# Two mixture-of-experts layers in one kernel: the second on gapless tiles of tokens, the first with a reordered start and earlier transposes

## The chip, the cores and the metric

The kernel runs on one core of a Trainium2 chip. Its time is device microseconds of one execution; before the change it is 2235.64 us, the median of three runs (2235.45 to 2235.82). A core has five engines that work side by side, each on a queue of its own: TensorE (PE in the profile; its weight loads are listed apart as PEld), VectorE (DVE), ScalarE (ACT), GpSimd (POOL) and SyncE (SP), which here only issues DMAs. A "q" behind an engine's name means its queue, where waits, register loads and DMA issues are handled.

## What is computed

The reference is a graph network of two layers over 2500 tokens of 256 features. Each layer adds a graph convolution and an attention block to the tokens and ends in a mixture of eight experts. What the change touches are the two expert parts:

```
# layer 0: each token takes its two best experts, unweighted
xn = layernorm(x)
idx = top_k(xn @ Wg + bg, 2)
h = gelu(einsum('td,edh->teh', xn, W1) + b1)          # W1: 8 x 256 x 512
y = einsum('teh,ehd->ted', h, W2) + b2                # W2: 8 x 512 x 256
x = x + sum of y over the two chosen experts

# layer 1: one shared first product, then one expert of eight
H = gelu(layernorm(x) @ W1 + b1)                      # W1: 256 x 1024
probs = softmax(H @ Wg + bg); e = argmax(probs)
x = x + probs[e] * (H @ Wd[e] + bd[e])                # Wd: 8 x 1024 x 256
```

All products are float32.

## The kernel before

Tokens lie on chip in `X`, 125 partitions by 20 blocks by 260 columns: 256 features and four columns for small facts such as mean, scale and the token's number. Five groups of four blocks (`NG`, `GT`) are the unit of most loops. Python writes the program in an order; a framework then orders the instructions on each engine's queue by their dependencies and by its own idea of when they are ready, so an instruction can stand earlier on its queue than the program has it. On the chip every queue is worked off in order.

**First expert layer.** `gates0(g, ...)` is a generator in three parts: statistics and normalized rows (lines 505 to 515), transposes and the choice of two experts (517 to 530), and slots and scatter (532 to 535). It runs for group g beside the aggregation of group g+1 (lines 664 to 701); for the last group all three parts run after the loop (711, 712). `take_slots` counts, with two small matmuls, how many tokens of each expert came before and so gives each token a row in the table `sorted0`, where each expert has a region of its own; `scatter` writes the rows with one indirect DMA of POOL for each block and choice (line 403). A fallback for lost edges follows as a loop of zero or one turns (line 715), which on these inputs is not entered but which every engine must pass. After it `pad` writes 128 empty rows behind each expert's tokens (eight DMAs of SP, line 491), and `plan` works out on VectorE which expert and which row each of the 47 tiles of 128 rows has (lines 414 to 436). Then, for each tile, `hidden` loads weights (`wt`) and rows (`xs`), transposes them into `px`, copies these to `xc`, forms the hidden products and the gelu `h`; `rest` forms the second product `py`, adds, and scatters to `back0`. The loop at lines 791 to 797 runs `hidden` one tile ahead of `rest`.

**Last expert layer.** A first pass (`gates`, `route`) forms H for all tokens, uses it for the gate alone, and scatters the rows by expert to `sorted1`. `pad` and `plan` follow as above, for 27 tiles: 20 would hold 2500 rows, and each of eight experts may leave its last tile partly empty. The second pass takes tiles in groups of three (`TG`): load, normalize to `xh`, transpose, eight products of 384 columns with gelu (lines 1256 to 1260), then for each tile eight products with its expert's matrix (line 1265), the sum `yo`, and an indirect DMA to the output (line 1271). Rows that are empty carry an index beyond the output and are dropped.

Of the kernel before, what the change touches and what calls it, by code (L numbers as in the profile page):

```python
# [10 lines left out]
I32 = mybir.dt.int32  # L11
# [28 lines left out]
NS1 = -(-N // TS) + NE - 1  # L40
# [8 lines left out]
def gps_kernel(ctx: ExitStack, tc: tile.TileContext, a, out):  # L49
# [45 lines left out]
    X = xpool.tile([P, NT, RW], F32, tag="X", name="X")  # L95
# [25 lines left out]
    slots = const.tile([P, NS0], F32, name="slots")  # L121
# [4 lines left out]
    region = const.tile([P, NE], F32, name="region")  # L126
# [241 lines left out]
    def one_best(pool, onehot, s):  # L368

        best = pool.tile([P, GT], F32, tag="best", name="best", bufs=2)  # L370
        V.tensor_reduce(best, s, AX.X, ALU.max)
        key = pool.tile([P, GT, NE], F32, tag="key", name="key", bufs=2)
        V.tensor_tensor(key, s, best[:, :, None].to_broadcast([P, GT, NE]), ALU.is_equal)
        V.tensor_tensor(key, key, rev[:, None, :].to_broadcast([P, GT, NE]), ALU.mult)
        first = pool.tile([P, GT], F32, tag="first", name="first", bufs=2)
        V.tensor_reduce(first, key, AX.X, ALU.max)
        V.tensor_tensor(onehot, key, first[:, :, None].to_broadcast([P, GT, NE]), ALU.is_equal)

    def take_slots(pool, mask, fill):


        flat = mask.rearrange("p i e -> p (i e)")
        ps = psum2.tile([P, 2, GT, NE], F32, tag="cx", name="ps")
        T.matmul(ps[:, 0].rearrange("p i e -> p (i e)"), below, flat, start=True, stop=True)  # L384
        T.matmul(ps[:, 1].rearrange("p i e -> p (i e)"), ones[:, :P], flat, start=True, stop=True)  # L385
        slot = pool.tile([P, GT, NE], F32, tag="slot", name="slot", bufs=2)
        for k in range(GT):
            V.tensor_tensor(slot[:, k, :], ps[:, 0, k, :], fill, ALU.add)  # L388
            V.tensor_tensor(fill, ps[:, 1, k, :], fill, ALU.add)
        return slot  # L390

    def slot_of(pool, slot, mask):

        t = pool.tile([P, GT, NE], F32, tag="pick", name="pick", bufs=2)
        V.tensor_tensor(t, slot, mask, ALU.mult)
        to = pool.tile([P, GT], I32, tag="to", name="to", bufs=4)
# [4 lines left out]
    def scatter(table, to, rows, moved):  # L401
        for k in range(GT):
            moved.append(G.indirect_dma_start(  # L403
                out=table, out_offset=bass.IndirectOffsetOnAxis(ap=to[:, k:k + 1], axis=0),
                in_=rows[:, k, :], in_offset=None,
# [4 lines left out]
    def plan(pool, fill, ns):  # L410
# [3 lines left out]
        V.tensor_tensor(tiles, fill, region, ALU.subtract)  # L414
# [7 lines left out]
        V.tensor_tensor(of, last[:, None, :].to_broadcast([P, ns, NE]), slots[:, :ns, None].to_broadcast([P, ns, NE]), ALU.is_le)  # L422
        who = pool.tile([P, ns], F32, name="who")
        V.tensor_reduce(who, of, AX.X, ALU.add)
        expert = pool.tile([P, ns], I32, name="expert")
# [3 lines left out]
        V.scalar_tensor_tensor(tiles, tiles, -float(TS), region, ALU.mult, ALU.add)  # L429
# [4 lines left out]
        V.scalar_tensor_tensor(who, slots[:, :ns], float(TS), who, ALU.mult, ALU.add)  # L434
        begin = pool.tile([P, ns], I32, name="begin")
        V.tensor_scalar(begin, who, float(NE * CAP), None, ALU.min)
        return expert, begin
# [39 lines left out]
    sorted1 = dram.tile([NE * CAP + TS, RW], F32, name="sorted1")  # L477
    back0 = dram.tile([2 * N, D], F32, name="back0")

    for table in (sorted0, sorted1):  # L480
        nc.scalar.dma_start(table[NE * CAP:NE * CAP + TS, :], empty)

    def pad(pool, table, empty, fill, moved):

        ends = pool.tile([P, NE], I32, name="ends")
        V.tensor_copy(ends, fill)
# [12 lines left out]
    fill0 = const.tile([P, NE], F32, name="fill0")  # L499
    V.tensor_copy(fill0, region)  # L500
    fill1 = const.tile([P, NE], F32, name="fill1")
    V.tensor_copy(fill1, region)

    def gates0(g, pool, moved):

        mv, rstd = norm_stats(X, g * GT, GT)
        rows = [pool.tile([P, GT, RW], F32, tag=f"rows{n}", name=f"rows{n}", bufs=2 - n) for n in range(2)]
# [203 lines left out]
    for _ in range(3):  # L711
        next(gating)
# [626 lines left out]
```

## Time and profile before

| what | us |
|---|---|
| median of three runs | 2235.64 |
| profiled execution, whole | 2239.74 |
| its span, on which all rows below are | 2238.0 |
| TensorE busy | 2009.1 |
| VectorE busy | 872.0 |
| ScalarE busy | 594.2 |
| GpSimd busy | 294.4 |
| last update of X before the first expert layer ends | 304.09 |
| first transpose of the first expert layer | 354.94 |
| its last scatter starts | 548.84 |
| last scatter to `sorted1` starts | 2010.72 |
| first product of the second pass | 2022.33 |
| last expert product ends, last scatter starts | 2230.45, 2231.71 |

Times within the span are microseconds from its start. A float32 matmul shows as two records in the trace, so a count of x16 is eight matmuls. The row "PEclk" of the page gives the clock granted to TensorE, in tenths of full speed: after an idle stretch it is half for some microseconds.

### The profile page before, as it was taken

What the parts mean: (1) busy time and instruction counts of PE and PEld (TensorE: products, weight loads), DVE (VectorE), ACT (ScalarE), POOL (GpSimd) and SP (SyncE); (2) the same over time, 40 slices, a digit from 0 to 9 for tenths busy, and PEclk for the clock granted to TensorE, in tenths of its full rate; (3) what the DMA queues carried; (4) which work ended last, traced back from release to release, by engine and by line L of the source; (5) the groups of instructions that cost most, each with busy time, mean ns of one, the idle gap of its engine ahead of it and who ended that gap; (6) DMA issues with size and microseconds to landing.
All of it is one profiled execution on the core that took longest, in us unless ns stands there. A gap on an engine that the chain in (4) does not pass through costs nothing. (4 is left out here: it accounts for less than half of the span.)

```text
span 2238.0 us, 25483 instructions
## 1 busy us (share of the span) xinstructions
PE 2009.1 (90%) x9145; PEld 1336.2 (60%) x9145; DVE 872.0 (39%) x2764; ACT 594.2 (27%) x1008; POOL 294.4 (13%) x265
## 2 busy tenths in 40 slices
PE   2799956997799999999999999999987997978998
PEld 2556635876476766676666676767643442326676
DVE  7866532332734463434525463443120003222111
ACT  1533202222533323232233324133110001332221
POOL 2303331222210000100001010011111000120111
PEclk9799977999899999999999999999989998988999
DMA  4113256664410001100110001100025336011110
GB/s 119 37 55 105 78 155 188 206 188 152 105 51 14 1 12 51 42 1 5 45 35 23 1 12 49 47 1 1 1 75 152 86 90 203 19 42 38 31 30 20
DMA packets 87295, 143.51 MB, mean 64 GB/s; under 512 B 18898, under 2 KB 69056, under 8 KB 86402
## 3 DMA queue, kind: packets, MB, share of 16 engines
q1 hardware_dynamic: 71233, 117.01, 18.0%
q0 software_dynamic: 12832, 18.28, 2.9%
q10 hardware_dynamic: 3093, 6.46, 1.1%
q8 instruction: 77, 1.26, 0.2%
q14 instruction: 60, 0.49, 0.1%
HBM read 104.84 MB, written 38.81 MB: 64 GB/s over the span
## 5 line engine op out<-in xcount | busy, mean ns | idle before, releaser
L1089 PE MATMUL mm<-w,h 128*125 128x256 f32 x1280 | 286.1, 379 | 0.0
L1079 PE MATMUL mm<-xT,w 128*128 128x500 f32 x640 | 283.2, 584 | 0.0
L288 PE MATMUL pa<-piece,table 125*128 125x500 bf16 x1200 | 269.8, 378 | 13.5 <-DVE t L852 5.6
L1089 PEld LDWEIGHTS mm<-w,h 128*125 128x125 f32 x1280 | 239.0, 188 | 43.2 <-issue 9.2
L288 PEld LDWEIGHTS <-table 125*128 125x128 bf16 x1200 | 117.7, 99 | 144.5 <-issue 17.8
L1079 PEld LDWEIGHTS mm<-xT,w 128*128 128x128 f32 x640 | 119.3, 191 | 112.6 <-issue 102.2
L1082 ACT ACTIVATE h<-mm,bf 128x500 f32<-128x500 f32 x160 | 107.1, 677 | 231.5 <-PE mm L1079 231.1
L288 PE MATMUL pa<-edges,xb 125*128 125x500 bf16 x600 | 134.2, 377 | 1.7 <-ACT edges L662 1.7
L1074 POOL TENSOR_TENSOR tok<-tok,b 125x1024 f32<-125x1024 f32 x20 | 47.3, 2365 | 584.6 <-DVE tok L1066 534.1
L1090 DVE TENSOR_TENSOR tok<-tok,mm 125x256 f32<-125x256 f32 x80 | 33.5, 418 | 210.0 <-PE mm L1089 169.3
L1257 PE MATMUL mm<-xc,w 128*128 128x384 f32 x288 | 102.1, 511 | 7.5 <-DVE xc L92 5.4
L765 PE MATMUL mm<-xc,wt 128*128 128x128 f32 x752 | 97.1, 283 | 7.5 <-DVE idx L771 4.3
L765 PEld LDWEIGHTS mm<-xc,wt 128*128 128x128 f32 x752 | 89.6, 194 | 17.8 <-DVE xc L761 12.4
L779 PE MATMUL py<-w,h 128*128 x376 | 96.0, 381 | 0.9 <-ACT h L769 0.9
L288 PEld LDWEIGHTS <-xb 125*128 125x128 bf16 x600 | 58.1, 100 | 63.8 <-issue 3.9
L1265 PE MATMUL mm<-wd,hs 128*128 x432 | 94.7, 379 | 0.0
L1055 DVE TENSOR_TENSOR tok<-tok,po 125x256 f32<-125x256 f32 x80 | 30.2, 414 | 154.4 <-PE po L1052 153.9
L769 ACT ACTIVATE h<-mm,wt 128x128 f32<-128x128 f32 x188 | 53.8, 368 | 137.3 <-issue 127.1
L1265 PEld LDWEIGHTS mm<-wd,hs 128*128 128x128 f32 x432 | 82.1, 190 | 13.1
L353 ACT ACTIVATE xT<-mm,mixc 128x500 f32<-128x500 f32 x80 | 58.9, 767 | 114.0 <-PE mm L348 79.8
L662 ACT CAST edges<-mm 125x500 bf16<-125x500 f32 x100 | 64.6, 784 | 88.9 <-PE mm L659 88.9
L1257 PEld LDWEIGHTS mm<-xc,w 128*128 128x128 f32 x288 | 55.4, 198 | 50.9 <-DVE xc L92 10.8
(325 smaller groups left out, 2832.2 us busy)
## 6 DMA issues: line engine op xcount, KB each, us to landing
wt<-in_expert_in_dram SPq DMA_DIRECT2D x47, 514.0 KB
piece<-adj SPq DMA_DIRECT2D x100, 218.8 KB
xs<-sorted SPq DMA_DIRECT2D x74, 130.0 KB
w<-in_L_mix_W_dram SPq DMA_DIRECT2D x8, 1024.0 KB
wd<-in_L_ffn_Wd_dram SPq DMA_DIRECT2D x8, 1024.0 KB
w<-in_L_ffn_W_dram SPq DMA_DIRECT2D x8, 512.0 KB
adj<-edges SPq DMA_DIRECT2D x2, 1750.0 KB
terms<-t SPq DMA_DIRECT2D x10, 336.0 KB
```

What stands on the lines that cost most here:

```text
L288: T.matmul(pa[c], table[:, k, n, c * 128:(c + 1) * 128], e, start=(k == 0 and n == 0), stop=(k == NT - 1 and n == 2))
L353: S.activation(o, ps, AF.Identity, bias=shift[:, c:c + 1], scale=gain[:, c:c + 1])
L662: S.copy(o.rearrange("p s (n d) -> p n s d", d=BD), ps[:P].rearrange("p (n s d) -> p n s d", n=BD, d=BD))
L765: T.matmul(ps[:, j * TS:(j + 1) * TS], wt[:, c * F0 + j * 128:c * F0 + (j + 1) * 128], xc[:, c * TS:(c + 1) * TS], start=(c == 0), stop=(c ...
L769: S.activation(h[:, j * TS:(j + 1) * TS], ps[:, j * TS:(j + 1) * TS], AF.Gelu, bias=wt[:, 2 * F0 + j:2 * F0 + j + 1])
L779: T.matmul(ps, h[:, j * TS:(j + 1) * TS], w2[:, ds(e, 1), j, :], start=(j == 0), stop=(j == NJ - 1))
L1074: G.tensor_tensor(o, o, b2[:P, None, :].to_broadcast([P, GT, D]), ALU.add)
L1079: T.matmul(ps, w1[:, c, j * 128:(j + 1) * 128], fT[:, c, g * GC:(g + 1) * GC], start=(c == 0), stop=(c == 1))
L1082: S.activation(h, ps, AF.Gelu, bias=bf[:, l, j:j + 1])
L1089: T.matmul(ps, hh[j][:, k * P:(k + 1) * P], w2[:, j, :], start=(j == 0), stop=(j == nj - 1))
L1257: T.matmul(ps[:, :nt * TS], w1[:, c, j * 128:(j + 1) * 128], xc[:, c, :nt * TS], start=(c == 0), stop=(c == 1))
L1265: T.matmul(ps, hs[j][:, k * TS:(k + 1) * TS], wd[:, ds(e, 1), j, :], start=(j == 0), stop=(j == nj - 1))
```

## The change

In the first expert layer:

- The last group's gate is split into two generators of two blocks each. The first starts when the first two of the four blocks have their final X. The two are advanced by hand in the order 0, 1, 0, 1, 1.
- Both row buffers, `rows0` and `rows1`, now exist twice (before, `rows1` once). Filling the small columns and the copy to `rows1` move from the first part of `gates0` to the third, for all groups.
- `pad` and `plan` run ahead of the fallback loop; the loop repeats them for its own result. The load of the bias table `brow` moves from ACT's queue to SP's.
- `hidden` is cut in two: `turned0` loads, transposes and copies; it runs a whole tile ahead of the products.

In the last expert layer:

- `sorted1` has no regions with gaps. Pairs of experts share a stretch of 2500 rows, one filling it upwards and the other downwards (`sign`, `begin1`). The table lies in memory that held the adjacency, and there are no empty rows any more.
- `visits` replaces `pad` and `plan`. It gives each of 2500 places in order of expert its row (`whence`) and owner (`own`), and lists 27 visits: pairs of a tile and an expert with rows in it.
- The second pass runs over 20 tiles without gaps, 2500 columns, in groups of 2, 2, 4, 4, 4 and 4. `fetch` gathers rows with POOL's indirect DMA into X's own memory; `inner` writes the gelu into a ring of twelve tiles (`hs`). For each visit `take` copies one tile of the ring, at a place known only at run time, to `taken`, and `visit` multiplies by the expert's matrix. Rows of the tile that belong to another expert get an index beyond the output.

The core of the diff:

```diff
-        rows = [pool.tile([P, GT, RW], F32, ..., bufs=2 - n) for n in range(2)]
...
+    def gate_rows(pool):
+        return [pool.tile([P, GT, RW], F32, tag=f"rows{n}", name=f"rows{n}", bufs=2) for n in range(2)]
...
+                    if g == NG - 1 and k == 1:
+                        rows = gate_rows(gate0)
+                        halves = [gates0(g, gate0, moved0, rows, lo, 2) for lo in (0, 2)]
+                        next(halves[0])
+                if g < NG - 1:
+                    gating = gates0(g, gate0, moved0, gate_rows(gate0))
+                else:
+                    for b in (0, 1, 0, 1, 1):
+                        next(halves[b])
...
-    nc.scalar.dma_start(brow.rearrange("p e n -> p (e n)"), row_bcast(a["L0_ffn_b2"], 0, NE * D, 128))
-    for _ in range(3):
-        next(gating)
+    nc.sync.dma_start(brow.rearrange("p e n -> p (e n)"), row_bcast(a["L0_ffn_b2"], 0, NE * D, 128))
+    pad(moe, sorted0, empty, fill0, moved0)
+    expert, begin = (moe.tile([P, NS0], I32, name=name) for name in ("expert", "begin"))
+    plan(moe, fill0, NS0, expert, begin)
...
-    pad(moe, sorted0, empty, fill0, moved0)
-    expert, begin = plan(moe, fill0, NS0)
...
-    ahead = hidden(0)
-    for t in range(1, NS0):
-        nxt_t = hidden(t)
-        rest(*ahead)
+    queue = [turned0(0)]
+    ahead = None
+    for t in range(NS0):
+        if t + 1 < NS0:
+            queue.append(turned0(t + 1))
+        nxt_t = hidden(*queue.pop(0))
+        if ahead is not None:
+            rest(*ahead)
         ahead = nxt_t
```

The new second pass and the two functions it turns on (`inner`, `turned` and the ends of `visits` are left out):

```diff
+    def visits(pool, fill, at):
+        turned_by, start = (v.rearrange("p k t -> p (k t)") for v in (sign, begin1))
+        count = pool.tile([128, NE], F32, name="count")
+        V.tensor_tensor(count, fill, start, ALU.subtract)
+        V.tensor_tensor(count, count, turned_by, ALU.mult)
+        ends = pool.tile([128, NE], F32, name="ends")
+        V.tensor_copy(ends, count)
+        for e in range(1, NE):
+            V.tensor_tensor(ends[:, e:e + 1], ends[:, e:e + 1], ends[:, e - 1:e], ALU.add)
...
+        V.tensor_tensor(whence, place_of, side, ALU.add)
...
+        def fetch(lo, hi):
+            for t in range(lo, hi):
+                m = rows_of(t)
+                G.indirect_dma_start(
+                    out=xs[:m, t, :], out_offset=None, in_=sorted1,
+                    in_offset=bass.IndirectOffsetOnAxis(ap=whence[:m, t:t + 1], axis=0),
+                )
...
+        def take(v):
+            r = nc.values_load(kept[0:1, v:v + 1], engines=[mybir.EngineType.DVE], ...)
+            h = fin2.tile([128, nj * TS], F32, tag="taken", name="taken")
+            V.tensor_copy(h, hs[:, ds(r, 1), :].rearrange("p o n -> p (o n)"))
+            return v, h
+
+        def visit(v, h):
+            e = expert_of(expert, v)
+            r = nc.values_load(which[0:1, v:v + 1], engines=[mybir.EngineType.DVE], ...)
+            ps = psum2.tile([128, D], F32, tag="cx", name="py")
             for j in range(nj):
+                T.matmul(ps, h[:, j * TS:(j + 1) * TS], wd[:, ds(e, 1), j, :], start=(j == 0), stop=(j == nj - 1))
+            row = xs[:, ds(r, 1), :].rearrange("p o n -> p (o n)")
+            idx = fin2.tile([128, 1], I32, tag="idx", name="idx", bufs=4)
+            far = fin2.tile([128, 1], F32, tag="far", name="far", bufs=4)
+            V.tensor_scalar(far, own[:, ds(r, 1)], expert_f[:, v:v + 1], float(1 << 20), ALU.not_equal, ALU.mult)
+            V.tensor_tensor(idx, far, row[:, D + 3:D + 4], ALU.add)
+            yo = fin2.tile([128, D], F32, tag="yo", name="yo", bufs=4)
+            V.tensor_tensor(yo, ps, bdf[:, ds(e, 1), :].rearrange("p o n -> p (o n)"), ALU.add)
+            V.scalar_tensor_tensor(yo, yo, row[:, D + 2:D + 3], row[:, :D], ALU.mult, ALU.add)
...
+        fetch(*groups[0])
+        fetch(*groups[1])
+        xc, n = turned(*groups[0])
+        taken = None
+        for u, (lo, hi) in enumerate(groups):
+            inner(lo, hi, xc, n)
+            for v in range(lo, hi if u + 1 < len(groups) else NV):
+                nxt_v = take(v)
+                if taken is not None:
+                    visit(*taken)
+                taken = nxt_v
+                if v == lo and u + 1 < len(groups):
+                    xc, n = turned(*groups[u + 1])
+            if u + 2 < len(groups):
+                fetch(*groups[u + 2])
+        visit(*taken)
```

## The prediction

> **What bounds the kernel now.** I read the page first, then tables of busy time by stretch, the timeline of the two expert layers, and the waits inside them. The page's slices show TensorE at 90% of the span, with two dents that the change touches: slices 6 and 7 (280 to 392 us, digits 5 and 6) and slices 36 and 37 (from 1958 us, digits 7 and 8).
>
> ```profile
> PE   2799956997799999999999999999987997978998
> PEclk9799977999899999999999999999989998988999
> ...
> L1257 PE MATMUL mm<-xc,w 128*128 128x384 f32 x288 | 102.1, 511 | 7.5 <-DVE xc L92 5.4
> L765 PE MATMUL mm<-xc,wt 128*128 128x128 f32 x752 | 97.1, 283 | 7.5 <-DVE idx L771 4.3
> L1265 PE MATMUL mm<-wd,hs 128*128 x432 | 94.7, 379 | 0.0
> ```
>
> The reader should see that each expert layer is TensorE work of 90 to 100 us a line with little waiting in front of it. So two things pay: fewer columns, and shorter holes. The hole ahead of the first expert layer is seen in the timeline (start, duration, engine and line, operation; in brackets the idle time before it and what ended it):
>
> ```profile
> 303.61 0.48 DVE L700 SCALAR_TENSOR_TENSOR X<-mm,rval,X 125x256 f32<-125x256 f32 x1
> 312.70 1.04 ACT L515 COPY rows<-rows 125x1024 f32<-125x1024 f32 x1 [15.88 <-DMA sorted<-rows,to]
> 314.27 3.53 PE L522 MATMUL pg<-wg,gT 128*125 128x8 f32 x16 [4.05 <-ACTq L715]
> 335.20 1.18 POOL L403 DMA_INDIRECT sorted<-rows,to  x1 [0.30 <-issue]
> 341.40 0.17 DVE L486 CAST ends<-fill 125x8 int32<-125x8 f32 x1 [17.40 <-DMA piece<-adj]
> 342.28 6.65 SPq L491 DMA_DIRECT2D sorted<-empty  x8
> 351.18 0.36 SPq L756 DMA_DIRECT2D xs<-sorted  x1
> 354.94 0.69 PE L759 MATMUL px<-ident,xs 128*128 128x128 f32 x2 [33.07 <-DMA xs<-sorted]
> ```
>
> From the last update of X (304.09) to the first transpose (354.94) is a chain of 50.9 us: statistics, gate, eight scatters on POOL at 1.49 us each, the fallback loop at L715 that lets nobody on before the scatters have landed (341.2), then the plan, eight empty-row loads and the first tile. Inside the two layers TensorE waits for these (waits by engine and line, us in total, times, longest; first 360 to 548 us, then 2016 to 2238 us):
>
> ```profile
> PE mm L765 <- DVE idx L771: 4.3, 3, 1.7
> PE mm L765 <- DVE xc L761: 2.7, 3, 1.1
> PE py L779 <- ACT h L769: 0.9, 3, 0.3
> ```
>
> ```profile
> DVE idx L1267 <- DMA out_dram<-yo,idx: 50.4, 23, 4.4
> PE mm L1257 <- DVE xc L92: 5.4, 5, 2.4
> ```
>
> The second fence holds a trap: VectorE stands 50.4 us before `idx`, waiting for a scatter to give a buffer back, and now and then the copy of `xc` is queued behind it.
>
> **A, the head of the first expert layer.** Three edits. (1) The last gate runs in two halves of two blocks, and the first starts after block 1 instead of 3. VectorE's small operations cost about 0.2 us whatever their width: variance and rsqrt are 11 operations in 2.9 us (304.81 to 307.66), the choice of two experts 13 in 2.9 us (317.84 to 320.7), pick and index 0.7 us. Halving pays these 6.5 us twice. Against it: about 2 us of the first half's statistics fit into gaps before 304.09; TensorE's transposes and gate products (2.06 and 3.53 us at half clock) and the evacuations now lie beside VectorE; and POOL starts its first four scatters early. Added up: rows of half one 307.5, of half two 311; products of half one 311.3; its choice 314.3; slots, pick, index 317; four scatters 317.7 to 323.7. Half two has its index at about 321, before POOL is free, so its last scatter starts at 323.7 + 3 x 1.49 = 328.2 instead of 335.2: 7.0 us. (2) The second buffer of `rows1` takes away ACT's 15.88 us wait above, behind which the copy of `gT` stood (313.65 instead of 310.3); that is inside the 7.0. (3) Plan and empty rows move ahead of the loop. On SP they stand behind eight W2 loads, the bias load that moves there from ACT (0.4 us of issue) and seven `piece` loads, all issued by 320.3; eight empties at 0.83 us then end at about 328, beside POOL's scatters. The plan (5.5 us of VectorE) hides there too. The path from the loop's end to the first tile's load falls from 9.8 us (341.4 to 351.18) to two register loads and one weight load, 1.9 us as between 348.93 and 351.18 less 0.8 us of waiting: about 8 us. Together 15.0. Bounds: 7 if halving gains nothing or an empty row that lands late holds the loop; 17 if the order is ideal. I take 14, near the sum, as all terms but the interleaving are rows. If the `piece` loads were queued between the empties, some 1.5 us would be lost.
>
> Gates of groups 0 to 3 run beside the aggregation, where TensorE is full; their row setup moves behind the choice, POOL 0.66 us and ACT 1.04 us ahead of scatters nobody waits for: nothing. Two constants and one memset more at the start, one DMA fewer: nothing.
>
> **B, transposes a tile ahead.** TensorE needs 26 records a tile, 3.8 us (276 records from 400 to 440 us). It runs 188 us with 179.6 busy; the three waits above are 7.9 of the 8.4 idle. With `px` a tile (3.8 us) ahead, its evacuation (0.42 us) and the `idx` copy before it have that much slack. What is late next is the load of `xs`: its issue follows the weight buffer of four tiles back by some 4.4 us and it lands 3.7 to 4.1 us later, against a need at about 11.2 us: 2.7 us to spare. Bounds 4 to 8.3; I take 7.
>
> **C, the last expert layer.** Work removed: 27 tiles of 128 columns become 2500 columns. L1257 spaces its records 0.322 us for 384 columns (10.3 us for 32), 0.839 ns a column; 32 records a column make 92.7 us before, 67.1 after: 25.6. Transposes 54 to 40, at 0.137 us (0.82 us for six): 1.9. Expert products stay 27 x 16 records at 0.219 us, 94.5 us.
>
> Start: before, last scatter 2010.72, empties until 2015.0, `xs` issued 2016.80, first product 2022.33. After: `visits` costs VectorE some 25 small operations to `whence`, 5.2 us, done by 2011.2, hidden by the scatters. The gathers sit on POOL behind the scatters and need them landed, 4.0 us after issue, so about 2015; each costs 1.19 + 0.3 us on POOL and lands in 4.1 (the `win` gather). Two tiles land at 2019.2 and 2020.7, products at about 2022.3: even, 2 us either way.
>
> Stalls before: 2022.33 to 2230.45 is 208.1 us for 193.8 of work, so 14.3 lost (7.5 idle, the rest half clock). After I count: half clock 2.5; the first `take` exposed 2.5; the transposes of group 2, whose four gathers wait for the first visit's result, need 1 + 6 + 4 us and have 10.4 of cover, 2 with order; VectorE's queue 4; other 2: 13. Later groups have 13.75 + 3.5 us of cover for the same 11. New on VectorE per visit: three register loads at 0.30 us, `far` and `idx` 0.15 each, `yo` 0.42 + 0.48, and the copy `take` of 1024 elements, which the trace lacks. Nearest row: 1.22 us (L931, 1024 elements at one a cycle). The Trainium skill, "VectorE: DVE Perf Modes", perf-mode tier table, gives a float32 SBUF copy twice that rate, from which I estimate 0.7 us. Between 0.7 and 1.25 I take 1.1, by the row. Sum 3.2 us beside TensorE's 3.5 a visit: it just fits.
>
> A rule speaks against this copy: "SBUF — State Buffer", SBUF: two separate sides, says that such a copy locks POOL out of the port with which it writes descriptors. The trace has POOL's indirect DMAs at 0.97 us with no such copy beside them, landing 2.4 us after issue. By the row a scatter costs its visit nothing; by the rule it may land up to one copy (1.1 us) later. Only where the next `idx` waits for that landing does it reach TensorE: 21 visits without cover x 1.1 = 23 us by the rule, 0 by the row. I take the 4 us above.
>
> C gives 27.5 + 14.3 - 13 = 28.8; I take 28. Bounds 12 to 39.
>
> **Sum.** 14 + 7 + 28 = 49. The profiled execution (span 2238.0, 2239.74 in all) becomes about 2190.7; it lies 4.1 above the median of the runs, 2235.64, so I forecast **2187**.
>
> **Rivals.**
> 1. *The loop or SP holds the head, or the gathers pace the tail* (A 7, C 12 to 20): 2235.6 - 7 - 7 - 15 = about 2207. For it: eight empties share SP with 13 other loads. Against: DMA share falls to 0.15 after 324 us.
> 2. *VectorE's queue takes the bound in C; slower.* If each `idx` waits for the scatter of the visit before, as in the 50.4 us above, the cycle is `yo` 0.95, POOL 0.25, landing 2.5 + 1.1 by the lock, `idx` 0.3, `take` with loads 1.6: 6.7 us instead of 3.5. 21 visits x 3.2 = 67 us, less the 4 counted: 2187 + 63 = 2250. It decides from a cycle of 5.8 us (49 / 21 + 3.5). Against: `take` can be queued before that `idx`; then the cycle is 4.0.
> 3. *Everything overlaps*: A 17, B 8, C 36: 2175.
>
> **Chances.** Forecast (2176 to 2198) 0.55; rival 1 and milder forms of 2 (2198 to 2231) 0.27; rival 3 0.10; no change 0.02; rival 2 0.06. A measurement here tells 0.2%, 4.5 us, from nothing. Faster 0.92, same 0.02, slower 0.06. Range 2170 to 2214: rival 3 below, most of rival 1 above.
>
> **What would show it.** First `px` at about 341 instead of 354.94, last L403 scatter near 328; TensorE idle inside the first layer under 2 us; the 128x384 group replaced by 512- and 256-wide ones with 67 to 70 us; visits 3.5 us apart at the end. Wrong: a first `px` after 347, visits over 4.5 us apart, or VectorE waiting for `out_dram` with TensorE waiting for `taken`.

## The result, and the profile after

The changed kernel takes **2210.59 us**, the median of four runs (2205.23 to 2213.28), beside 2235.73 us of the kernel before in the same comparison: a ratio of 0.9884, with a 95% interval of 0.9863 to 0.9906. The gain is 25 us, about half of the 49 forecast. The time lies inside the range 2170 to 2214 and near the first rival's 2207.

The profiled execution takes 2208.22 us, with a span of 2205.4. That is 31.5 us less than the profiled execution before, which was itself 4.1 us above its median, while this one is 2.4 below: the traces differ by 6.5 us more than the medians do. I split the difference of the spans at three events found in both traces: the first transpose and the last scatter of the first expert layer, and the start of the last product that forms H for the gate (`mm<-xTf,w`), ahead of the second pass. The table calls this one the last gate product:

| stretch, us | before | after | gain |
|---|---|---|---|
| start to the first transpose of the first expert layer | 354.9 | 346.5 | 8.4 |
| from there to that layer's last scatter | 193.9 | 198.7 | -4.8 |
| from there to the last gate product (nothing is edited here) | 1447.3 | 1442.8 | 4.5 |
| from there to the end of the span | 241.9 | 217.4 | 24.5 |

So the last layer brings nearly all of it. The first layer starts 8.4 us earlier and gives more than half of that back before it ends. These are the rows of the page of the changed kernel that answer to those shown before:

```profile
PE   2799967998699999999999999999987897995997
...
L1394 PE MATMUL py<-wd,taken 128*128 x432 | 100.1, 390 | 8.8 <-DVE taken L1384 8.8
L851 PE MATMUL mm<-xc,wt 128*128 128x128 f32 x752 | 97.5, 283 | 10.2 <-DVE xc L841 8.8
...
L863 PE MATMUL py<-w,h 128*128 x376 | 94.2, 380 | 0.0
```

Two numbers matter. L851, the hidden product of the first layer, waits 10.2 us in all, 8.8 of them for the copy of `xc`; before, with the transposes in the same tile, its row had 7.5 in all. And L1394, the expert product of the last layer, waits 8.8 us for `taken`, an operation that did not exist before.

**The head.** The timeline of the changed kernel around the last gate (start, duration, engine, line, operation; in brackets the idle time before it):

```profile
296.97 1.03 PE L767 MATMUL mm<-wx,xT 128*125 128x256 f32 x4
...
304.78 0.48 DVE L771 SCALAR_TENSOR_TENSOR X<-mm,rval,X 125x256 f32<-125x256 f32 x1
...
318.63 1.19 POOL L407 DMA_INDIRECT sorted<-rows,to  x1 [11.78 <-issue]
...
323.06 8.63 SPq L546 DMA_DIRECT2D sorted<-empty  x8
...
329.10 1.19 POOL L407 DMA_INDIRECT sorted<-rows,to  x1 [0.30 <-issue]
...
339.62 0.37 SPq L836 DMA_DIRECT2D xs<-sorted  x1
...
346.48 0.69 PE L839 MATMUL px<-ident,xs 128*128 128x128 f32 x2 [25.67 <-SPq L499]
```

The last scatter starts at 329.10 (forecast 328.2, before 335.20), the eight empty rows lie beside the scatters, and between the loop, which SP leaves at 337.9, and the first load of rows there are 1.7 us. But SP is held in the loop until 8.8 us after the last scatter's start; before, SP left it after 5.2 us and VectorE, on which the plan waited, after 6.0. And the first transpose comes 6.9 us after the load of its rows is issued instead of 3.8.

**A tile of the first layer.** TensorE's part of the timeline, where the change works as it is written:

```profile
389.40 0.38 PE L839 MATMUL px<-ident,xs 128*128 128x128 f32 x2
389.62 1.95 PE L851 MATMUL mm<-xc,wt 128*128 128x128 f32 x16
391.41 1.89 PE L863 MATMUL py<-w,h 128*128 x8
393.14 0.38 PE L839 MATMUL px<-ident,xs 128*128 128x128 f32 x2
...
396.87 1.95 PE L851 MATMUL mm<-xc,wt 128*128 128x128 f32 x16
398.66 1.89 PE L863 MATMUL py<-w,h 128*128 x8
400.39 0.38 PE L839 MATMUL px<-ident,xs 128*128 128x128 f32 x2
400.61 0.60 PE L863 MATMUL py<-w,h 128*128 x2
```

The transposes `px` of one tile stand right before the products `mm` of the tile before: a tile takes 393.14 - 389.40 = 3.74 us. Then, at 396.87, an `mm` follows with no `px` ahead of it, and the next `px` lands inside the batch of second products. From there on the queue has the old shape; the timeline of all engines, some tiles later:

```profile
434.86 0.38 PE L839 MATMUL px<-ident,xs 128*128 128x128 f32 x2
...
435.06 0.48 DVE L866 SCALAR_TENSOR_TENSOR yo<-py,xs,brow 128x256 f32<-128x256 f32 x1 [2.95 <-PE py L863]
435.08 1.03 PE L863 MATMUL py<-w,h 128*128 x4
...
435.58 0.48 DVE L868 SCALAR_TENSOR_TENSOR yo<-xs,yo 128x256 f32<-128x256 f32 x1
435.99 0.42 DVE L841 COPY xc<-px 128x256 f32<-128x256 f32 x1
...
436.46 2.05 PE L851 MATMUL mm<-xc,wt 128*128 128x128 f32 x16 [0.35 <-DVE xc L841]
...
439.21 0.38 PE L839 MATMUL px<-ident,xs 128*128 128x128 f32 x2
```

The transposes are done at 435.2, but VectorE has the two sums `yo` of the tile before in its queue ahead of `xc`, 435.06 to 436.0, and TensorE runs dry. A tile takes 439.21 - 434.86 = 4.35 us. The kernel before had `px` in the same place, between four and four records of `py`, but in VectorE's queue `xc` stood between the two sums `yo`, with only one of them ahead of it:

```profile
402.22 0.38 PE L759 MATMUL px<-ident,xs 128*128 128x128 f32 x2
402.43 0.48 DVE L782 SCALAR_TENSOR_TENSOR yo<-py,xs,brow 128x256 f32<-128x256 f32 x1 [2.56 <-PE py L779]
402.44 1.03 PE L779 MATMUL py<-w,h 128*128 x4
...
402.83 0.42 DVE L761 COPY xc<-px 128x256 f32<-128x256 f32 x1
403.17 0.48 DVE L784 SCALAR_TENSOR_TENSOR yo<-xs,yo 128x256 f32<-128x256 f32 x1
403.31 2.05 PE L765 MATMUL mm<-xc,wt 128*128 128x128 f32 x16
...
406.06 0.38 PE L759 MATMUL px<-ident,xs 128*128 128x128 f32 x2
```

`xc` is done at 403.25 and TensorE goes on at 403.31: 3.84 us a tile. It did not hold this to the end: it has 276 records from 400 to 440 us and 254 from 440 to 480, which at 26 a tile is 3.8 and 4.1 us. So the changed kernel is 0.1 us a tile faster while it has the lead, up to tile 13, then up to 0.5 slower while the kernel before is still at its pace, and little different at the end.

### The profile page after: what moved, and what is told of

It reads as the page before. It is cut to its first block, busy times and chain, and to the rows that moved or that the text cites. A ratio compares the mean times of both kernels' runs of the same rounds, so it can differ in the third digit from the quotient of the medians.

```text
span 2205.4 us, 25369 instructions
## 1 busy us (share of the span) xinstructions
PE 1981.8 (90%) x9039; PEld 1317.9 (60%) x9039; DVE 892.8 (40%) x2854; ACT 582.3 (26%) x991; POOL 316.1 (14%) x292
## 5 line engine op out<-in xcount | busy, mean ns | idle before, releaser
L292 PE MATMUL pa<-piece,table 125*128 125x500 bf16 x1200 | 268.7, 377 | 13.2 <-DVE t L940 5.7
L1394 PE MATMUL py<-wd,taken 128*128 x432 | 100.1, 390 | 8.8 <-DVE taken L1384 8.8
L851 PE MATMUL mm<-xc,wt 128*128 128x128 f32 x752 | 97.5, 283 | 10.2 <-DVE xc L841 8.8
L851 PEld LDWEIGHTS mm<-xc,wt 128*128 128x128 f32 x752 | 90.0, 195 | 23.8 <-DVE xc L841 20.7
L1394 PEld LDWEIGHTS py<-wd,taken 128*128 128x128 f32 x432 | 83.5, 195 | 24.9 <-DVE taken L1384 11.4
L1078 PE MATMUL mm<-xT,wa 128*128 128x500 f32 x160 | 76.1, 619 | 4.0 <-ACT xT L357 3.9
L1289 PE MATMUL mm<-xTf,w 128*128 128x500 f32 x160 | 78.4, 613 | 0.0
```

What stands on the lines that cost most here:

```text
L292: T.matmul(pa[c], table[:, k, n, c * 128:(c + 1) * 128], e, start=(k == 0 and n == 0), stop=(k == NT - 1 and n == 2))
L851: T.matmul(ps[:, j * TS:(j + 1) * TS], wt[:, c * F0 + j * 128:c * F0 + (j + 1) * 128], xc[:, c * TS:(c + 1) * TS], start=(c == 0), stop=(c ...
L1078: T.matmul(ps, wk[:, kc, c * 128:(c + 1) * 128], hT[:, kc, g * GC:(g + 1) * GC], start=(kc == 0), stop=(kc == 1))
L1289: T.matmul(ps, w1[:, c, j * 128:(j + 1) * 128], xT[:, c, g * GC:(g + 1) * GC], start=(c == 0), stop=(c == 1))
L1394: T.matmul(ps, h[:, j * TS:(j + 1) * TS], wd[:, ds(e, 1), j, :], start=(j == 0), stop=(j == nj - 1))
```

## The experiments

All times are medians against the same kernel before, which stood at 2235.6 to 2237.7 us in these comparisons. Runs of one changed kernel lie 5 to 12 us apart, so differences below 4 us are read from traces, not from medians. A table collects, for the first expert layer, in how many of the 46 later tiles `px` is queued ahead of the `mm` of the tile before, or (in the first three, except in lead_forced) in the midst of it, and the events in the trace. "Last group" is the start of the first product `mm<-wx,xT` (L767; L696 before) that goes into the last group's X. What whole_gate, plan_late and bias_on_act edit lies behind it, and yet the traces reach it between 294.5 and 298.3 us. So times in the head are best counted from it.

| kernel | median, us | tiles with the lead | last group | first `px` | last scatter of the layer | between |
|---|---|---|---|---|---|---|
| before | 2235.6 | 0 | 296.0 | 354.9 | 548.8 | 193.9 |
| last_only | 2211.95 | 0 | 294.9 | 354.8 | 548.3 | 193.5 |
| lead_undone | 2206.12 | 0 | 297.8 | 347.9 | 545.8 | 197.9 |
| after | 2210.59 | 13 | 297.0 | 346.5 | 545.2 | 198.7 |
| whole_gate | 2211.75 | 13 | 294.5 | 341.7 | 543.8 | 202.1 |
| bias_on_act | 2206.96 | 13 | 295.9 | 345.7 | 543.6 | 197.9 |
| plan_late | 2206.72 | 23 | 294.8 | 347.7 | 542.4 | 194.7 |
| lead_forced | 2190.46 | 46 | 298.3 | 348.0 | 530.2 | 182.2 |
| xs_first | 2189.30 | 46 | 296.2 | 342.4 | 525.6 | 183.2 |

### last_only: the first layer as before, the last layer changed

All edits of the first expert layer are taken back: the gate of the last group in one piece, small columns in its first part, one `rows1`, plan and empties behind the loop, the bias on ACT's queue, and

```diff
-    queue = [turned0(0)]
-        if t + 1 < NS0:
-            queue.append(turned0(t + 1))
-        nxt_t = hidden(*queue.pop(0))
+        nxt_t = hidden(*turned0(t))
```

> The change of the last expert layer alone: the first expert layer has its whole gate, its one buffer for the second rows, its plan behind the loop, its bias load on ACT and its transposes beside their own tile, as before. Theory (from the traces, the last layer brought 24 to 25 us of the second pass and the first layer 4 to 5 in all): 2211 to 2215 us. Rival (the prediction's shares, 28 and 21): the whole change is at 2210.6, so this would lie near 2208 only if the first layer brought nothing; at 2220 or more the first layer brought 10 us.

2211.95 us (2204.99 to 2217.3, six runs), ratio 0.9878 (0.9855 to 0.9901): within the spread the same as the whole change. The first layer's edits together are worth about 1 us by the medians and 3.1 us by the end of the layer in the traces (548.3 against 545.2), or 5.2 us counted from the last group. The last layer alone carries the gain.

### lead_forced and lead_undone: is it the order of TensorE's queue?

lead_forced keeps the program and adds an ordering edge, so that a tile's products are queued behind the next tile's transposes; lead_undone puts `turned0` and `hidden` together again, and nothing else.

```diff
-            T.transpose(px[:, c * TS:(c + 1) * TS], xs[:, c * 128:(c + 1) * 128], ident)
+            turn = T.transpose(px[:, c * TS:(c + 1) * TS], xs[:, c * 128:(c + 1) * 128], ident)
+        turns.append(turn.ins)
...
-        nxt_t = hidden(*queue.pop(0))
+        with tc.issue_after(turns[-1]):
+            nxt_t = hidden(*queue.pop(0))
```

and lead_undone:

```diff
-        if t + 1 < NS0:
-            queue.append(turned0(t + 1))
-        nxt_t = hidden(*queue.pop(0))
+        nxt_t = hidden(*turned0(t))
```

> The changed kernel, with one ordering edge for each tile: TensorE may not start a tile's hidden products before the next tile's two transposes have been queued. In the changed kernel's trace the first thirteen tiles of the first expert layer run with the transposes a tile ahead at 3.735 us each, and from the fourteenth on the transposes stand just ahead of their own tile's products again and a tile takes 4.3 us. Theory (the lead is lost by the order of the queue, not by the chip): all 47 tiles at 3.74 us, the stretch from first transpose (346.5) to last scatter (545.2) falls from 198.7 to about 184 us, the kernel by about 15 us. Rival (the rows really arrive too late for a tile of lead): TensorE then waits for xs instead of xc, and the stretch stays within 4 us of 198.7.

> The changed kernel with load, transposes and products of a tile written together again, as before the change. Theory (the lost lead is what made the layer slower): the stretch from first transpose to last scatter of the first expert layer returns to about the 193.9 us of the kernel before, so the kernel gains about 5 us. Rival (the layer is slower for another reason, such as the second row buffer or the moved bias load): the stretch stays near 198.7 us.

lead_forced: 2190.46 us (2186.94 to 2192.72), ratio 0.9784 (0.9748 to 0.982), 20 us under the change. The stretch falls from 198.7 to 182.2 us. lead_undone: 2206.12 us (2204.71 to 2213.63), ratio 0.9856 (0.9821 to 0.9891), no slower than the change, with a stretch of 197.9. So the transposes a tile ahead bring nothing as the change has them (198.7 beside 197.9). Where the queue really holds them ahead they bring 15.7 us against lead_undone, and 11.7 against the kernel before, which is what my bounds of 4 to 8.3 were about.

lead_undone's own theory failed: without any lead the stretch does not return to 193.9. Its tiles are written as those of last_only, where the stretch is 193.5. last_only keeps 3.84 us a tile up to tile 20, lead_undone only up to tile 13, with 4.36 in the three tiles behind it. So some 4 us of the longer stretch come with the edits of the head, not with the lost lead; which of them does it, and by what, no run here shows.

Why the lead is worth more than the waits it ends can be read from the two tile shapes above: a tile without the lead costs 4.35 - 3.74 = 0.61 us more, and only 0.35 of it is listed as waiting. The other 0.26 hides in busy time: batches cut in two (two of `py` at 1.03 instead of one at 1.89) and a batch after a stall that takes 2.05 instead of 1.95. Some 30 such tiles make 18 us, about the 16.5 us by which the stretch falls from after to lead_forced.

### xs_first: the rows loaded ahead of the weights

```diff
+        xs = moe2.tile([128, RW], F32, tag="xs", name="xs", bufs=5)
+        nc.sync.dma_start(xs, tile_rows(sorted0, begin, t))
         wt = moe2.tile([128, 2 * F0 + NJ], F32, tag="wt", name="wt", bufs=4)
         nc.sync.dma_start(wt, a["expert_in"][ds(e, 1)].rearrange("o p n -> (o p) n"))
-        xs = moe2.tile([128, RW], F32, tag="xs", name="xs", bufs=5)
-        nc.sync.dma_start(xs, tile_rows(sorted0, begin, t))
```

> The changed kernel with each tile's rows (130 KB) loaded ahead of its weights (514 KB) on SP's queue. In the changed kernel the first rows land 6.8 us after issue, with one tile's weights issued 0.9 us ahead of them. Theory (they stand behind the weights in the same rings): the first transpose comes 2 to 3 us earlier than 346.5. Rival (the traffic of other queues, the broadcast loads of POOL and the last adjacency loads, sets it): under 1 us.

2189.30 us (2182.27 to 2191.18), ratio 0.9772 (0.9744 to 0.9801). I had expected an earlier first `px` and no more, and the larger effect was a surprise: two lines swapped do what the edge did. All 46 tiles hold the lead, as TensorE's part of the timeline of xs_first shows at 433 us,

```profile
432.99 0.38 PE L839 MATMUL px<-ident,xs 128*128 128x128 f32 x2
433.20 1.95 PE L851 MATMUL mm<-xc,wt 128*128 128x128 f32 x16
...
436.72 0.38 PE L839 MATMUL px<-ident,xs 128*128 128x128 f32 x2
```

3.73 us a tile. And the first `px` comes 4.2 us after its rows are issued instead of 6.9 (4.7 in xs_idx, which has the same edit); counted from the last group it is 3.3 us earlier. A load that is issued behind a 514 KB weight load is late twice: on the chip, and in the framework's plan of the queue, which puts `px` where it expects the rows to be there. That the plan's guess is the link between the swap and the order is inferred: what is seen is that the order of the queue changes with the swap.

### whole_gate, plan_late, bias_on_act: the three edits of the head

whole_gate puts the last gate into one piece again, plan_late moves `pad` and `plan` behind the fallback loop, bias_on_act gives the load of `brow` back to ACT's queue:

```diff
-                    if g == NG - 1 and k == 1:
-                        rows = gate_rows(gate0)
-                        halves = [gates0(g, gate0, moved0, rows, lo, 2) for lo in (0, 2)]
-                        next(halves[0])
+                gating = gates0(g, gate0, moved0, gate_rows(gate0))
```

```diff
-    pad(moe, sorted0, empty, fill0, moved0)
...
-    plan(moe, fill0, NS0, expert, begin)
...
+    pad(moe, sorted0, empty, fill0, moved0)
+    plan(moe, fill0, NS0, expert, begin)
```

```diff
-    nc.sync.dma_start(brow.rearrange("p e n -> p (e n)"), row_bcast(a["L0_ffn_b2"], 0, NE * D, 128))
+    nc.scalar.dma_start(brow.rearrange("p e n -> p (e n)"), row_bcast(a["L0_ffn_b2"], 0, NE * D, 128))
```

> The changed kernel with the last group's gate in one piece again, after all four blocks have their final X, both row buffers kept, plan and empty rows still ahead of the loop. In the changed kernel the gate's last scatter starts 23.8 us after the last update of X (305.26 to 329.10; before the change 31.1 us) and the first transpose is at 346.5. Theory (the halves shift the scatters, and these the loop's end): last scatter and first transpose come 5 to 7 us later. Rival (the empty rows, not the scatters, set the end of the loop): last scatter 5 to 7 us later, first transpose under 3 us later.

> The changed kernel with plan and empty rows behind the loop again (the loop no longer repeats them). Theory of the prediction: they cost 8 us on the path, so the first transpose comes about 8 us later than 346.5. Rival (the loop is left later because the empty rows stand in front of it, and the first rows land later because nothing spaces the loads: 5 of the 8 us are given back): the loop is left about 2 us earlier relative to the last scatter, the first rows land 3.7 us after their issue as before, and the first transpose comes only 3 to 4 us later.

> The changed kernel with the 1 MB bias table loaded from ACT's queue again instead of SP's. In the changed kernel the loop is left at about 337 us, 7.8 us after the last scatter of the gate starts (before: 5.9), and the first rows land 6.8 us after their load is issued (before: 3.7). Theory (the table stands in SP's queue ahead of the eight empty-row loads, which hold the loop): the loop is left 1.5 to 2 us earlier and the kernel gains about 2 us. Rival (the traffic is the same whichever queue carries it): no change beyond 1 us.

whole_gate 2211.75 us (2207.71 to 2213.92), plan_late 2206.72 (2202.78 to 2211.47), bias_on_act 2206.96 (2202.38 to 2209.72): none is told apart from the change by more than its spread. The traces say more, if they are counted from the last group. The timeline of whole_gate has

```profile
294.50 1.03 PE L767 MATMUL mm<-wx,xT 128*125 128x256 f32 x4
...
330.73 1.19 POOL L407 DMA_INDIRECT sorted<-rows,to  x1 [0.30 <-issue]
...
341.71 0.69 PE L833 MATMUL px<-ident,xs 128*128 128x128 f32 x2 [24.91 <-DMA xs<-sorted]
```

Without halves the last scatter starts 36.23 us after the last group's first product, with them 32.13 us, and before the change 39.16 us. So of the 7.0 us the halves give 4.1, and 2.9 come from what both versions share, the second row buffer and the fill and copy moved to the third part of the gate; that share wasn't run by itself. The first `px` is nevertheless 2.3 us earlier without halves (47.2 us after that product, not 49.5). Its empties are all issued by 327.3 us, 3.4 us ahead of the last scatter, where the change issues the last of them 2.3 us after it. SP leaves the loop 6.2 us after the last scatter's start instead of 8.8, and `px` follows the issue of its rows by 3.1 us instead of 6.9. This run's theory had the first `px` 5 to 7 us later and its rival less than 3 us later; that it comes earlier, neither said.

With the plan late, SP leaves the loop 5.2 us after the last scatter's start (332.5 after 327.3), as before the change, and not 8.8: the empties issued ahead of the loop do hold it. The first `px` is 3.5 us later (53.0 us, not 49.5), as the rival had it, though not by its sum: `px` follows the issue of its rows by 5.7 us and not by 3.7. Moving the bias load leaves every event of the head within 0.5 us of where it was, as its rival had it. And in all of these the layer ends at 542 to 546: where the queue has no full lead, an earlier first `px` is paid back in the stretch. From last_only to whole_gate `px` moves by 12.8 us and the end by 4.1.

### idx_12: more buffers for the index of a visit

```diff
-            idx = fin2.tile([128, 1], I32, tag="idx", name="idx", bufs=4)
-            far = fin2.tile([128, 1], F32, tag="far", name="far", bufs=4)
+            idx = fin2.tile([128, 1], I32, tag="idx", name="idx", bufs=12)
+            far = fin2.tile([128, 1], F32, tag="far", name="far", bufs=12)
```

> The changed kernel with twelve buffers instead of four for idx and far in the visits of the last expert layer. In the changed kernel the last group's visits start 4.87 us apart, and VectorE stands about 2.6 us in each of them at idx, until the scatter just issued has landed and given a buffer back. Theory (that wait is the bound): visits of the last group go to TensorE's 3.5 us, TensorE's 8.8 us of waiting for taken fall under 2, the kernel gains 9 to 10 us. Rival (VectorE's own work and register loads, or the copy taken, bound the visits): under 3 us.

2195.62 us (2191.41 to 2196.89), ratio 0.9807 (0.9771 to 0.9844), 15 us under the change. What it removes is seen in the timeline of the changed kernel, late in the last layer:

```profile
2159.33 0.48 DVE L1402 SCALAR_TENSOR_TENSOR yo<-yo,X 128x256 f32<-128x256 f32 x1
...
2160.09 0.97 POOL L1403 DMA_INDIRECT out_dram<-yo,idx  x1 [3.88 <-DVE far L1398]
2162.53 0.16 DVE L1399 TENSOR_TENSOR idx<-far,X 128x1 int32<-128x1 f32 x1 [2.59 <-DMA out_dram<-yo,idx]
...
2163.59 0.69 DVE L1384 COPY taken<-hs 128x1024 f32 x1 [0.51 <-issue]
2164.20 0.48 DVE L1402 SCALAR_TENSOR_TENSOR yo<-yo,X 128x256 f32<-128x256 f32 x1
...
2164.34 3.72 PE L1394 MATMUL py<-wd,taken 128*128 x16 [1.15 <-DVE taken L1384]
```

It is a ring: the scatter at 2160.09 must land, 2.44 us later, before VectorE writes the next `idx` (2162.53), behind which `taken` stands in the same queue, behind which TensorE waits 1.15 us; the `yo` that follows releases the next scatter. One turn is 2164.20 - 2159.33 = 4.87 us against 3.5 us of products. This `idx` is not that of the visit at hand. It is the 22nd, written when 18 scatters have been issued: the framework queues `idx` four visits ahead, as far as the buffers reach, and so makes it wait for the newest scatter. With twelve buffers all 27 are written by 2134.9 us, ahead of the last group's first visit, and the timeline of idx_12 has no such wait,

```profile
2150.96 0.48 DVE L1402 SCALAR_TENSOR_TENSOR yo<-yo,X 128x256 f32<-128x256 f32 x1
2151.72 0.97 POOL L1403 DMA_INDIRECT out_dram<-yo,idx  x1 [2.54 <-DVE yo L1402]
...
2153.86 0.69 DVE L1384 COPY taken<-hs 128x1024 f32 x1 [0.61 <-issue]
2154.47 0.48 DVE L1402 SCALAR_TENSOR_TENSOR yo<-yo,X 128x256 f32<-128x256 f32 x1
```

and a visit takes 2154.47 - 2150.96 = 3.51 us: TensorE is the bound. On the page of idx_12 the product's row is

```profile
L1394 PE MATMUL py<-wd,taken 128*128 x432 | 95.1, 380 | 1.0 <-DVE taken L1384 1.0
```

The wait falls by 7.8 us and the busy time by 5.0 for the same 432 records. Together 12.8, of the 13.2 us by which the stretch from the gate's last product to the end gets shorter (217.4 to 204.2). As in the first layer, a good part of what a stall costs stands in the busy column. Here most of it is the clock, as the timeline of the changed kernel shows:

```profile
2041.82 5.41 PE L1394 MATMUL py<-wd,taken 128*128 x16 [1.94 <-DVE taken L1384]
```

Two visits, behind the longest waits of 1.94 and 2.05 us, take 5.41 us instead of 3.62; the granted clock is 0.50 from 2042.2 to 2045.2 and from 2175.4 to 2178.4 us. That is 3.6 of the 5.0 us. Behind the five shorter waits, 0.57 to 1.15 us, the clock stays at 1.00 and a visit takes 3.72.

Not all of the 13 us is the ring. The visit at 2041.82 stands behind the late gathers of the second group; in idx_12 its wait is 0.97 us and the clock stays up, which is some 2.7 us. Whether four buffers would do if `idx` were kept in its own visit wasn't run.

### lead_idx, xs_idx, xs_idx_whole: do the gains add?

The three combine the edits above: lead_forced with idx_12; xs_first with idx_12; and the latter with the last gate in one piece.

> The queue order held by an edge (as in lead_forced, 2190.46 us) and 12 buffers of idx and far (as in idx_12, 2195.62 us) in one kernel. Theory: the two stalls lie in different layers and nothing lies between them that could take either back, so the gains against after's 2210.59 add, 20.1 + 15.0: 2175.5 us. Rival, part of both gains is the drift of the middle of the program between kernels: 2182 or more.

> Rows loaded ahead of weights in turned0 (as in xs_first, 2189.3 us) and 12 buffers of idx and far (as in idx_12). Theory, the gains add: 2189.3 - 15.0 = 2174.3 us; the first layer ends by 526 us and the last expert products run about 204 us from the end of the gate's products to the end of the span. Rival, they overlap in drift: 2181 or more.

> As xs_idx, with the last gate in one piece again. In whole_gate the first transpose came 4.8 us earlier than in after but the layer ended at the same time, because the order of TensorE's queue lost the lead. Here the order holds the lead, so theory says an earlier first transpose now counts: if loading xs first already takes the early start (342.4 us in xs_first), then the pieces are worth nothing: within 2 us of xs_idx. Rival, halves do help once TensorE is the bound: xs_idx is faster by the 1.6 us by which its last scatter is earlier, or more, up to 5 us.

| kernel | median, us (five runs) | ratio to before | first `px` | end of the layer | gate's end to end |
|---|---|---|---|---|---|
| lead_idx | 2178.77 (2174.36 to 2180.63) | 0.9747 (0.9734 to 0.976) | 345.0 | 526.2 | 204.1 |
| xs_idx | 2178.50 (2172.79 to 2180.86) | 0.9745 (0.9731 to 0.9759) | 342.9 | 525.5 | 204.1 |
| xs_idx_whole | 2178.94 (2175.38 to 2184.3) | 0.9752 (0.9733 to 0.977) | 340.3 | 523.7 | 203.9 |

In the traces the gains add fully: the ends of both stretches are those of the single experiments. By the medians the sum is 3 to 4 us short of the theory's 2175.5 and 2174.3, between theory and rival, and that is within what separates runs of one kernel. The page of xs_idx shows what is left of the first layer's wait:

```profile
L851 PE MATMUL mm<-xc,wt 128*128 128x128 f32 x752 | 94.5, 280 | 2.5 <-DMA wt<-in_expert_in_dram 2.5
...
L863 PE MATMUL py<-w,h 128*128 x376 | 88.8, 380 | 0.0
```

Two lines that move two loads, and two buffer counts, make the change worth 57 us instead of 25. And xs_idx_whole repeats the question of the halves where the lead is held. Counted from the last group (295.9 us in xs_idx, 295.5 here), the last scatter is 3.7 us later without halves, the first `px` 2.2 us earlier and the end of the layer 1.5 us earlier. So here an early start does count; the medians do not tell it. The halves can go: they bring the scatters forward, as meant, but in both pairs of traces the first transpose is later with them.

## Why the prediction was right and wrong

**What was right.** The sign; that the last layer is the larger part; and most of that layer's sum. The time lies in the range because the range was wide: 49 us were forecast and 25 came, all three terms were too large, and 2210.59 lies outside the 2176 to 2198 that was held most likely. Two of the three signs that the prediction named for being wrong are there: visits 4.87 us apart, and VectorE waiting for `out_dram` with TensorE waiting for `taken`.

C was taken at 28 and measured at 24.5 us. The columns came out as counted: by shape, the first product's groups in the changed kernel are

```profile
L1370 PE MATMUL mm<-xc,w 128*128 128x512 f32 x96 | 41.7, 592 | 0.0
L1370 PE MATMUL mm<-xc,w 128*128 128x256 f32 x64 | 16.9, 422 | 1.4 <-DVE xc L94 0.8 <-ACT xc L92 0.7
L1370 PE MATMUL mm<-xc,w 128*128 128x452 f32 x32 | 12.3, 542 | 0.0
```

41.7 + 16.9 + 12.3 = 70.9 us of busy time, where the row before had 102.1 (busy times overlap at their ends; the 67 to 70 forecast for these groups is missed by a little). The start of the second pass was even, as said: 25.0 us from the gate's last product to the first product, 26.2 before. The pass itself fell from 208.1 to 183.2 us, against 179.3 by the sum.

**C, the term that was mis-sized: 4 us for VectorE's queue.** More buffers take 13 away (idx_12). The mechanism was named, in the second rival: `idx` waiting for the landing of the scatter just issued, with `take` behind it. I took 4 us because `take` could be queued ahead of that `idx`. It is not, because the framework puts `idx` four visits early, and the ring has 4.87 us a turn, between the 4.0 of the mild form and the 6.7 of the full one. Of the 1.8 us between 4.87 and 6.7, 1.2 are the landing: it takes 2.44 us where I had 3.6, the lock's delay of 1.1 included. And TensorE waits in six visits of the last group, not in 21. The other terms of the 13 us of stalls were too large: the pass has 183.2 - 166.3 = 16.9 us above its work, so without the 13 some 4 are left for half clock, first `take`, group 2 and the rest, for which I had 9. That C came as near as it did is in part luck, since these two errors lie in opposite directions.

**The copy `take`.** I took 1.1 us by the nearest row and kept 0.7 as the lower bound, by the Trainium skill, "VectorE: DVE Perf Modes", perf-mode tier table. The tile's row in the changed kernel's trace sides with the page:

```profile
L1384 DVE COPY taken<-hs x27: 684/694/695, 2023.8 to 2189.6; 128x1024 f32 x27
```

(shortest, median and longest in ns.) The row I leaned on, 1.22 us for 1024 elements, was an operation on two tensors; the float32 copy within SBUF took 0.69 us for as many.

**The rule on POOL's port.** I weighed 23 us by the Trainium skill, "SBUF — State Buffer", SBUF: two separate sides, against 0 by the row, and took the row. Both were seen. One of 27 scatters was issued while a `take` ran, in the timeline of the changed kernel:

```profile
2189.56 0.68 DVE L1384 COPY taken<-hs 128x1024 f32 x1
2189.59 1.51 POOL L1403 DMA_INDIRECT out_dram<-yo,idx  x1 [3.60 <-DVE yo L1402]
```

1.51 us instead of 0.97. The same pair stands in lead_forced (1.50) and in every other kernel with four buffers, always at this place of the program; with twelve no scatter is issued beside a `take`. Four other scatters were issued while a copy `xc`, which reads PSUM, had some 0.3 us to run, and took 1.00 to 1.02. So the runs agree with the rule for the copy within SBUF, at 0.54 us a collision. It was worth nothing here, because the ring spaces scatter and `take` apart: the scatter waits for the second `yo`, the `take` has run before it.

**B, the step that failed.** I took 7 us, for `px` a tile ahead gives its evacuation 3.8 us of slack. The slack is real where `px` is ahead in every tile, and then worth 11.7 us against the kernel before. But that the program calls `turned0(t + 1)` first does not put it first in TensorE's queue. In the changed kernel it stands first for 13 tiles of 46. My working named the late thing, the load of `xs` behind the weights, and counted 2.7 us to spare on the chip; it did not ask what the framework, which orders the queue ahead of time, makes of the same lateness. The kernel's description in this document says that the order is its own. Here, as with `idx` in the last layer, the order in the program could not be taken for the order in the queue, and for `px` the rivals had no case for it. The stretch grew by 4.8 us instead of shrinking by 7: 11.8 us of the miss. Of these, 7.8 are B's own, by lead_undone: it lost 0.8 us where 7 were forecast. The other 4.0 are the lengthening that comes with the edits of the head and that no term of the sum had; its cause stays open.

**A, 14 us forecast, 8.4 at the first `px`, less at the end.** Counted from the last group it is 9.4. The 7.0 for the halves and the second row buffer came out as 7.0 (39.16 to 32.13 us, 4.1 of it from the halves). The loop-to-load path became 1.7 us; the 1.9 of the working is not what its own figures give (351.18 - 348.93 - 0.8 = 1.45), but the saving of about 8 is right (8.3). What the sum left out was the price of the empties' place, named only as the lower bound: issued among the last scatters, they hold the loop 2.8 us longer (SP's 8.8 us against VectorE's 6.0), and the first `px` follows the issue of its rows 3.1 us later. The moved loads were counted on their queue, not for what waits for their landing. 7.0 + 8.3 - 2.8 - 3.1 = 9.4.

**The first rival** gave 2207 for A halved and gathers that pace the last layer. Its half about the head is what happened (A 8.4 for 7). Its half about the gathers is not: C is 24.5, not 12 to 20, and after the first group TensorE's direct waits for gathered rows sum to 1.0 us. So the measured time lies near this rival's 2207 by luck: the loss that it has in the gathers is in the transposes. The third rival's 36 us for C is what the layer gives with the buffers it needs: 24.5 + 13.2 = 37.7.

**What stays open.** The part between the two layers, which no experiment edits, lies between 1441.0 and 1449.6 us in the traces. It covers differences below 5 us between medians, and nothing here explains it. Nor does anything explain why the traces reach the last group of the first layer up to 4 us apart.

## What to carry to other kernels

Software pipelining in the program is only a wish where a framework orders the queues: compare the order of each engine's queue with what was meant, for every turn of the loop and not for the first few, and issue the load that a pipeline's head needs ahead of the large one that its tail needs. A buffer given back by a DMA's landing costs the whole landing in an in-order queue, with all that stands behind it; before moving work, ask whether a few more of a 512-byte tile end the wait. Count the events of two traces from a point that the edit cannot move, or drift will be read as gain. And the price of a stall is not the wait column alone: the busy column carried 5.0 us of 12.8 in one place and 0.26 of 0.61 in the other.

## What the runs showed of the hardware

- TensorE's work after a wait is slower, and how much depends on the wait: in the changed kernel a visit of 16 records of L1394 takes 3.62 us without a wait, 3.72 after waits of 0.57 to 1.15 us at a granted clock of 1.00, and 5.41 after waits of 1.94 and 2.05 us, with the clock at 0.50 for some 3 us. Where between 1.15 and 1.94 us the step lies, and what else sets it, the runs don't show.
- A scatter by POOL that starts with a copy within SBUF on VectorE takes 1.51 us; all others, beside the end of a copy out of PSUM too, take 0.97 to 1.02.
- From the issue of the first load of 130 KB of rows to the first transpose it is 6.5 to 6.9 us in the six kernels with halves, the empty rows ahead of the loop and the weight load ahead of the rows. It is 4.2 and 4.7 us with the weight load behind it (xs_first, xs_idx), 3.1 with the last empty row issued ahead of the last scatter (whole_gate), and 2.2 with both (xs_idx_whole). But it is 3.8 us in the kernel before and 5.8 in last_only, which have the same order of loads there, so 2 us of such a difference can be chance.
